# Two graph layers on one core: layer 0's row-by-entry matrix kept as bytes, and the seams around it reordered

## The chip, the cores and the metric

The kernel runs on one core of a Trainium2 chip. The metric is the device time of one execution in microseconds (us). The core's engines each run their own queue in order: TensorE (PE; PEld is its loading of weights), VectorE (DVE), ScalarE (ACT), GpSimd (POOL) and SyncE (SP). ACT, POOL and SP also issue DMAs, which share the core's 16 DMA engines.

## The reference

Input x is 4096 rows of 512 numbers, adj a 4096 by 4096 matrix of 0 and 1 that is about one in a thousand ones. Cut to what matters:

```python
# layer 0: attention with 8 heads over the neighbours in adj
Wh = einsum('nf,hfo->hno', x, W)
e  = leaky_relu(f1[:, :, None] + f2[:, None, :], 0.2)   # f1 = Wh.a[:64], f2 = Wh.a[64:]
e  = where(adj > 0, e, -9e15)
x  = layernorm(x + heads_side_by_side(softmax(e) @ Wh))
# layer 1: own row and mean of the neighbours
agg = (adj > 0) @ x / max(deg, 1)
out = concat(x @ W_self + b_self, agg @ W_nb + b_nb) @ W_comb + b_comb
x   = layernorm(x + relu(out))
```

## The kernel before

The 4096 rows are 32 blocks of 128. adj is not multiplied with anything: it is read once, and each row's few neighbours are turned into a list of column numbers. Both layers then gather their neighbours' rows from tables in HBM (t0 for layer 0, t1 for layer 1) with indirect DMAs. A block gathers 5 sets of 128 rows: the first three neighbours of each row (K0 = 3), and two sets of 128 shared entries (KH = 2) that hold the fourth and further neighbours of whatever rows have them. The order of all work is written out by hand: every engine runs its instructions in the order in which the code issues them.

**The adj stage** (loop at L778 over blocks 0 to 29). load_adj (L366) requests a block of adj as two half-blocks of 1 MB each on SP's queue; there are four buffers, so two blocks are under way. mask_adj (L375) turns a half-block into bf16 on ACT (L377). key_bank (L381) puts column numbers into a PSUM bank, fold_adj (L389) multiplies the masks with powers of two into the bank (L395), max_keys (L405) takes each row's largest keys on DVE (L410). Beside this, transposed (L307) turns a block of x (L311 on PE, the copy xT at L313 on ACT), node_block (L755) makes that block's table row (L319 on PE, copies to SBUF at L323 on DVE, two row buffers), and store sends it to t0.

**decode** (L412) works on four blocks at a time and is a generator, whose parts other work is put between. Part A (L417 to L430) unpacks keys; part B (L434 to L438) takes each block's sixteen largest; part C (L440 to L450) makes degrees and the first three indices; part D (L452 to L469) makes, for each of the four blocks, the 128 by 256 row-by-entry matrix (L465, L466), which says which row owns which shared entry; part E multiplies it with the lists (L473) and makes the shared entries' indices. With slow=True, used for the last four blocks, part D is split by block. "some(lists)" runs one part of each pending decode; in the loop each iteration runs one.

**The seam before layer 0** (L812 to L858): the last two node blocks, the masks and keys of blocks 30 and 31 (LB = 30), the gathers of blocks 0 and 1, the product of W_nb with the lower half of W_comb into m2 (fold_weights, L252: transposes L259, matmuls L270, copies L261 and L273), the last decode up to part C, and fold_bias (L276), which multiplies b_nb with the same half of W_comb on PE (L285) and adds it to a row of the bias on DVE (L289).

**Layer 0** (loop at L864). Step i works on several blocks at once: moments and normalizing of block i (L611, L618 to L627), the product with m2 of block i-1 (a_z, L632, its input turned by L311 and L313) and its store to t1, the weighted sums of block i+1, and the weights of block i+2. a_owners (L507) makes the entry-by-row matrix of a block from its lists; a_owned (L529) transposes it on PE (L532) and copies the result from PSUM to the tile st on ACT (L534); a_reach (L564) multiplies st with the reciprocal sums (L568), which the weights in a_normed need. Parts D and E of the last decode run in steps 2 to 6. Gathers go out of five buffers (GA = 5).

**The seam before layer 1** (L903 to L939): fold_weights for W_self into m1, fold_bias for b_self, spread_bias (L292), which spreads the one bias row over 128 rows by a matmul (L295).

**Layer 1** (loop at L941): gathers from t1 out of seven buffers, the product with m1 (L656), the shared entries (L663), the bias, normalizing (root, norm) and the store to the output.

Of the kernel before, what the change touches and what calls it, by code (L numbers as in the profile page):

```python
# [46 lines left out]
U32 = mybir.dt.uint32  # L47

K0 = 3
KH = 2  # L50
# [36 lines left out]
def listed_layers(  # L87
# [115 lines left out]
    oner = const.tile([1, P], F32, name="oner")  # L203
    nc.vector.memset(oner, 1.0)
# [13 lines left out]
    f1s = const.tile([P, NB, KS, H], F32, name="f1s")  # L218
    idx = const.tile([P, NB, KS], U32, name="idx")
# [32 lines left out]
    def fold_weights(loaded, m, wp, tag):  # L252
# [12 lines left out]
        for c in range(FB):  # L265
# [3 lines left out]
            for d in range(FB):  # L269
                nc.tensor.matmul(  # L270
                    mp, lhsT=wT[:, d, :], rhs=wc[:, d, :], start=(d == 0), stop=(d == FB - 1)
                )
            nc.scalar.copy(m[:, c, :], mp)  # L273
            wT = nxt

    def fold_bias(loaded, brw):  # L276
# [3 lines left out]
        bcol = small.tile([P, FB], F32, name="bcol", bufs=1)  # L280
        nc.scalar.copy(bcol, bt)
        yield
        bp = ps.tile([1, HD], F32, name="sm", bufs=2)
        for d in range(FB):
            nc.tensor.matmul(  # L285
                bp, lhsT=bcol[:, d : d + 1], rhs=loaded[1][:, d, :],
                start=(d == 0), stop=(d == FB - 1),
            )
        nc.vector.tensor_add(brow[0:1, :], bp, brow[0:1, :])  # L289
        yield  # L290

    def spread_bias():  # L292

        bp = ps.tile([P, HD], F32, name="sm", bufs=2)
        nc.tensor.matmul(bp, lhsT=oner, rhs=brow[0:1, :], start=True, stop=True)  # L295
# [38 lines left out]
    def mean_row(w_sb, xacc, wp):  # L334
# [9 lines left out]
        mr = wp.tile([P, HD], F32, name="y", bufs=2)  # L344
# [15 lines left out]
        nc.scalar.dma_start(t0[1:2, H:TW], mr[0:1, :])  # L360
# [5 lines left out]
    def load_adj(b, ap, hs=range(NH)):  # L366

        for h in hs:
# [6 lines left out]
    def mask_adj(b, h, ap):  # L375
        ab = masks[b, h] = ap.tile([P, NG // NH, SC], BF16, name="ab", bufs=3)
# [35 lines left out]
    def decode(b0, dp, place, slow=False):  # L412
# [26 lines left out]
        yield  # L439
# [21 lines left out]
        for b in range(b0, b0 + G):  # L461
# [4 lines left out]
            nc.vector.scalar_tensor_tensor(st, io, off, lt, OP.is_ge, OP.mult)  # L466
            sts.append(st)
# [61 lines left out]
    def a_owned(b, wp):  # L529
        tq = ps.tile([P, KH, P], F32, name="sm", bufs=2)  # L530
        for k in range(KH):
            nc.tensor.transpose(tq[:, k, :], OWN[b][:, k, :], ident)  # L532
        ST[b] = wp.tile([P, KH, P], F32, name="st", bufs=2)
        nc.scalar.copy(ST[b], tq)  # L534
# [157 lines left out]
    dp = ctx.enter_context(tc.tile_pool(name="decode", bufs=1, side="right"))  # L692
    fp_cm = tc.tile_pool(name="fold", bufs=1, side="right")
    fp = fp_cm.__enter__()
    ap_cm = tc.tile_pool(name="lists", bufs=1, side="right")
# [25 lines left out]
    for k in range(2):  # L721
        pa.append(ps.tile([P, HD], F32, name=("sm", "key")[k], bufs=(2, 1)[k]))
        nc.tensor.matmul(pa[k], lhsT=oner, rhs=av[0:1, k], start=True, stop=True)
# [50 lines left out]
    for h in range(NH):  # L774
        mask_adj(0, h, ap)
# [581 lines left out]
```

## Time and profile before

| what | value |
|---|---|
| median of three runs | 719.69 us (718.86 to 720.13) |
| the profiled execution: its run | 720.06 us |
| the profiled execution: its span | 718.4 us |
| mean granted TensorE clock | 0.965 of full speed |
| busy: PE, DVE, ACT, POOL | 646.3, 488.8, 443.7, 360.5 us |
| layer 0, 300 to 400 us: PE, DVE, ACT, POOL busy | 97.44, 92.43, 62.37, 65.79 of 100 us |
| layer 1, 600 to 700 us: PE, DVE, ACT, POOL busy | 100.00, 59.29, 72.09, 75.63 of 100 us |
| adj stage, 100 to 200 us: DMA | 392 GB/s |

A line of the timeline or of the groups gives the engine, the line of the kernel, the operation and "out<-in" by the names of tiles, then shapes; in a timeline it begins with the start and the duration in us, and in brackets stands how long the engine had been idle before it and what ended that. "issue" means that nothing shown was waited for. A busy PE is not a PE at its peak, since the ends of matmuls are modelled.

### The profile page before, as it was taken

The numbers are of one execution on the slowest core, as the hardware profiler recorded it, in microseconds if no ns is written. First come the engines' busy times: TensorE is split into PE (matmuls) and PEld (weight loads), VectorE is DVE, ScalarE is ACT, GpSimd is POOL, SyncE is SP. The second block draws the span as 40 slices with busy tenths as digits, with TensorE's granted clock in tenths as the row PEclk, the third lists the DMA queues.
The fourth block names the chain that finished last, engine by engine and source line by source line (L and its number), as shares of the span: only waits on it lengthen the run. The fifth ranks groups of instructions, "written<-read, shape, count | busy, mean of one in ns | idle before, by whom it ended". The sixth has DMA issues, their size and how long they took to land. (4 is left out here: it accounts for less than half of the span.)

```text
span 718.4 us, 9039 instructions
## 1 busy us (share of the span) xinstructions
PE 646.3 (90%) x2534; PEld 365.2 (51%) x2534; DVE 488.8 (68%) x1424; ACT 443.7 (62%) x915; POOL 360.5 (50%) x403
## 2 busy tenths in 40 slices
PE   4797888887999769999999999999999999999992
PEld 2465666655676335555555555554344444444440
DVE  5266777875876378999999999981116665566553
ACT  3567777676784315556666576664237777677764
POOL 6512222121002476566666666400777777777770
PEclk9989999999999978999999999999989999999997
DMA  9999999999997676977877887611667888888883
GB/s 282 389 352 394 393 393 394 393 391 392 390 391 265 216 211 204 316 213 206 231 228 231 232 227 230 185 44 45 200 203 245 258 254 260 254 258 258 262 255 108
DMA packets 84263, 191.28 MB, mean 266 GB/s; under 512 B 12513, under 2 KB 12521, under 8 KB 84206
## 3 DMA queue, kind: packets, MB, share of 16 engines
q0 software_dynamic: 25600, 84.56, 40.2%
q1 hardware_dynamic: 53952, 97.53, 37.0%
q10 hardware_dynamic: 4654, 8.54, 3.1%
q8 instruction: 22, 0.36, 0.2%
q14 instruction: 35, 0.29, 0.1%
HBM read 165.29 MB, written 25.31 MB: 265 GB/s over the span
## 5 line engine op out<-in xcount | busy, mean ns | idle before, releaser
L515 POOL DMA_INDIRECT g<-t,idx x320 | 304.4, 951 | 172.4 <-issue 120.2
L377 ACT ACTIVATE ab<-at 128x2048 bf16<-128x2048 int32 x64 | 122.3, 1911 | 55.8 <-DMA at<-in_adj_dram 49.6
L319 PE MATMUL pw<-w_sb,xT 128*128 128x264 f32 x512 | 133.4, 407 | 1.0 <-DVE row L323 0.9
L632 PE MATMUL pw<-m,xT 128*128 128x512 f32 x256 | 118.0, 604 | 3.1 <-ACT xT L313 1.7
L319 PEld LDWEIGHTS pw<-w_sb,xT 128*128 128x128 f32 x512 | 96.4, 198 | 29.3 <-issue 4.7
L313 ACT COPY xT<-tp 128x512 f32<-128x512 f32 x80 | 46.3, 579 | 91.5 <-PE tp L311 89.8
L305 POOL TENSOR_TENSOR xacc<-xacc,xs 128x512 f32<-128x512 f32 x32 | 41.1, 1284 | 122.6 <-DMA xs<-in_x_dram 122.0
L583 DVE TENSOR_TENSOR g<-g,key 128x1024 f32<-128x1024 f32 x64 | 77.9, 1217 | 1.1
L632 PEld LDWEIGHTS pw<-m,xT 128*128 128x128 f32 x256 | 46.1, 190 | 55.3 <-issue 45.8
L595 PE MATMUL nm<-g,own 128*128 128x512 f32 x128 | 66.3, 643 | 0.0
L656 PE MATMUL nm<-m,xT 128*128 128x512 f32 x128 | 60.4, 617 | 1.3 <-ACT xT L313 1.3
L311 PEld LDWEIGHTS tp<-ident,xs 128*128 128x128 f32 x320 | 40.9, 148 | 36.1 <-issue 29.8
L656 PE MATMUL pw<-m,xT 128*128 128x512 f32 x128 | 57.6, 593 | 0.0
L311 PE MATMUL tp<-ident,xs 128*128 128x128 f32 x320 | 50.6, 283 | 6.0 <-DMA xs<-in_x_dram 5.8
L323 DVE COPY row<-pw 128x264 f32<-128x264 f32 x64 | 27.1, 425 | 33.3 <-PE pw L319 23.9
L656 PEld LDWEIGHTS nm<-m,xT 128*128 128x128 f32 x128 | 24.1, 199 | 26.1 <-issue 24.6
L670 DVE SCALAR_TENSOR_TENSOR sm<-y,lst,nm 128x512 f32<-128x512 f32 x16 | 12.1, 755 | 36.7 <-PE nm L663 36.6
L670 DVE SCALAR_TENSOR_TENSOR sm<-y,lst,pw 128x512 f32<-128x512 f32 x16 | 12.1, 755 | 34.3 <-PE pw L663 34.3
L656 PEld LDWEIGHTS pw<-m,xT 128*128 128x128 f32 x128 | 23.2, 191 | 23.4 <-issue 23.4
L663 PE MATMUL pw<-g,own 128*128 128x512 f32 x64 | 31.4, 615 | 3.0 <-DMA g<-t,idx 3.0
L595 PEld LDWEIGHTS nm<-g,own 128*128 128x128 f32 x128 | 23.1, 200 | 16.9 <-issue 16.1
L549 PEld LDWEIGHTS sm<-e,own 128*128 128x128 f32 x128 | 19.8, 199 | 22.7 <-ACT e L543 11.6
(178 smaller groups left out, 1031.1 us busy)
## 6 DMA issues: line engine op xcount, KB each, us to landing
at<-in_adj_dram SPq DMA_DIRECT2D x64, 1024.0 KB, 11.2
t<-row SPq DMA_DIRECT2D x32, 256.0 KB, 3.6
out_dram<-row SPq DMA_DIRECT2D x32, 256.0 KB, 3.8
t<-row ACTq DMA_DIRECT2D x31, 260.0 KB, 6.0
xs<-in_x_dram SPq DMA_DIRECT2D x31, 256.0 KB, 11.5
g<-t,idx POOLq DMA_INDIRECT x320, 4.1
wc<-in_L_gnn_W_comb_dram SPq DMA_DIRECT2D x2, 1024.0 KB, 14.8
w_sb<-in_L_gnn_W_dram SPq DMA_DIRECT2D x8, 128.0 KB, 4.4
```

The source lines that it names most:

```text
L305: nc.gpsimd.tensor_tensor(xacc, xacc, xs[:, b, :], OP.add)
L311: nc.tensor.transpose(tp[:, c, :], xs[:, b, ts(c, P)], ident)
L313: nc.scalar.copy(t, tp)
L319: nc.tensor.matmul(pw, lhsT=xT[:, c, :], rhs=w_sb[:, c, k * HW : (k + 1) * HW], start=(c == 0), stop=(c == FB - 1),)
L323: nc.vector.tensor_copy(row[:, k * HW : (k + 1) * HW], pw)
L377: nc.scalar.activation(ab, loads.pop((b, h)), AF.Relu, accum_out=asum[:, b, h : h + 1])
L515: nc.gpsimd.indirect_dma_start(out=g[:, k, 0 : table.shape[1]], out_offset=None, in_=table[:, :], in_offset=bass.IndirectOffsetOnAxis(ap=i ...
L583: nc.vector.tensor_tensor(gv if to is None else to.rearrange("p (k h d) -> p k h d", k=1, h=H), gv, E[b][:, sl].unsqueeze(3).to_broadcast( ...
L595: nc.tensor.matmul(NM[b], lhsT=OWN[b][:, k, :], rhs=G0[b][:, K0 + k, H:TW], start=False, stop=(k == KH - 1), skip_group_check=True,)
L632: nc.tensor.matmul(pz, lhsT=xT[:, c, :], rhs=m2[:, c, :], start=(c == 0), stop=(c == FB - 1))
L656: nc.tensor.matmul(NM[b], lhsT=xT[:, c, :], rhs=m1[:, c, :], start=False, stop=False, skip_group_check=True,)
L663: nc.tensor.matmul(NM[b], lhsT=OWN[b][:, k, :], rhs=g[:, K0 + k, 0:HD], start=False, stop=(k == KH - 1), skip_group_check=True,)
```

## The change

In decode, each row-by-entry matrix is also copied to bytes by ACT, into a new tile "of" for all 32 blocks. In layer 0, a_owned no longer transposes: it copies the bytes back to numbers, from SBUF. Part B of a slow decode is split by block. fold_weights stops twice for each of its four column blocks where it stopped once. The bias: a column of b_nb or b_self is made once (bias_column), fold_bias multiplies it with the half of W_comb on DVE and adds up in all 128 rows of brow (cleared at block 3), and one matmul with ones sums the rows and spreads the result (sum_bias). The mean row uses a row buffer instead of a y buffer. Both halves of block 30 are requested in the loop, and block 30's masks run before the last fold of the loop's blocks. The buffers of adj and of the masks are pools of their own, and layer 0's small tiles come from a new pool (wq). In the seam and in layer 0's loop the order is as in the diff.

```diff
+    of = const.tile([P, NB, KH * P], U8, name="of")
...
                 nc.tensor.matmul(
                     mp, lhsT=wT[:, d, :], rhs=wc[:, d, :], start=(d == 0), stop=(d == FB - 1)
                 )
+            yield
             nc.scalar.copy(m[:, c, :], mp)
...
+    def bias_column(k, brw):
         bt = ps.tile([P, FB], F32, name="sm", bufs=2)
         nc.tensor.transpose(bt, brw, ident[0:FB, 0:FB])
...
+    def fold_bias(loaded, bcol):
         for d in range(FB):
-            nc.tensor.matmul(
-                bp, lhsT=bcol[:, d : d + 1], rhs=loaded[1][:, d, :],
-                start=(d == 0), stop=(d == FB - 1),
-            )
-        nc.vector.tensor_add(brow[0:1, :], bp, brow[0:1, :])
+            nc.vector.scalar_tensor_tensor(
+                brow, loaded[1][:, d, :], bcol[:, d : d + 1], brow, OP.mult, OP.add
+            )
-    def spread_bias():
+    def sum_bias():
         bp = ps.tile([P, HD], F32, name="sm", bufs=2)
-        nc.tensor.matmul(bp, lhsT=oner, rhs=brow[0:1, :], start=True, stop=True)
+        nc.tensor.matmul(bp, lhsT=ones, rhs=brow, start=True, stop=True)
         nc.scalar.copy(brow, bp)
...
-        mr = wp.tile([P, HD], F32, name="y", bufs=2)
+        mr = wp.tile([P, FW], F32, name="row", bufs=2)
...
             nc.vector.max(nb[:, g, 8:16], kj[:, g, :])
-        yield
+            if slow or g == G - 1:
+                yield
...
             nc.vector.scalar_tensor_tensor(st, io, off, lt, OP.is_ge, OP.mult)
+            nc.scalar.copy(of[:, b, :], st)
...
     def a_owned(b, wp):
-        tq = ps.tile([P, KH, P], F32, name="sm", bufs=2)
-        for k in range(KH):
-            nc.tensor.transpose(tq[:, k, :], OWN[b][:, k, :], ident)
         ST[b] = wp.tile([P, KH, P], F32, name="st", bufs=2)
-        nc.scalar.copy(ST[b], tq)
+        nc.scalar.copy(ST[b].rearrange("p k c -> p (k c)"), of[:, b, :])
...
-            load_adj(LB, ap, (0,))
+            load_adj(LB, ap)
         if b == 3:
             brw = load_bias(1)
+            nc.vector.memset(brow, 0.0)
...
+        if b == 5:
+            bcol = bias_column(1, brw)
...
     row = node_block(w, xT)
     store(w, row)
+    key_bank(LB)
+    for h in range(NH):
+        mask_adj(LB, h)
     fold_adj(LB - 1, dp)
     max_keys(LB - 1)
     row = node_block(w + 1, nxt)
     store(w + 1, row, nc.sync)
-    load_adj(LB, ap, (1,))
     load_adj(LB + 1, ap)
...
     m2s = fold_weights(loaded, m2, wp, "pw")
-    next(m2s)
-    mask_adj(LB, 0, ap)
-    some(lists)
-    next(m2s)
-    key_bank(LB)
-    mask_adj(LB, 1, ap)
-    some(lists)
-    next(m2s)
     some(lists)
     fold_adj(LB, dp)
     max_keys(LB)
-    a_owners(0, wp)
-    a_owned(0, wp)
-    mask_adj(LB + 1, 0, ap)
     next(m2s)
     key_bank(LB + 1)
-    mask_adj(LB + 1, 1, ap)
+    some(lists)
+    for k in range(3):
+        next(m2s)
+    mask_adj(LB + 1, 0)
+    a_owners(0, wp)
+    fold_bias(loaded, bcol)
+    some(lists)
+    mask_adj(LB + 1, 1)
+    next(m2s)
     fold_adj(LB + 1, dp)
     max_keys(LB + 1)
+    next(m2s)
...
+    wq = ctx.enter_context(tc.tile_pool(name="work2", bufs=1))
+    a_owned(0, wq)
...
     lists = [decode(NB - G, dp, on_last, slow=True)]
     some(lists)
-    next(m2s, None)
-    some(lists)
-    for _ in fold_bias(loaded, brw):
-        pass
-    some(lists)
...
+        if i == -1:
+            next(m2s)
         if i >= -1 and on(i + 2):
-            a_owned(i + 2, wp)
+            a_owned(i + 2, wq)
...
+        if i == -2:
+            next(m2s)
+            some(lists)
...
+        if i == -1:
+            next(m2s, None)
-        if 2 <= i < 8:
+        if 2 <= i < 12:
             some(lists)
...
+    bcol = bias_column(0, brw)
+    fold_bias(loaded, bcol)
     for _ in fold_weights(loaded, m1, wp, "nm"):
         pass
-    for _ in fold_bias(loaded, brw):
-        pass
-    spread_bias()
+    sum_bias()
```

## The prediction

> **What bounds the kernel now.** I read the busy table by stretches first, then the timeline of each seam, the waits, and the chain that ended last. Three stages show: up to about 224 us the stream of adj (388 to 395 GB/s in every window from 60 to 215 us); layer 0 to 498 us; layer 1 to the end.
>
> The chain of waits that ended last, and the waits in layer 1 (engine, tile, line, released by: us, times, longest):
> ```profile
> 698.63 1.00 POOL g L515
> 699.94 5.19 DMA g<-t,idx
> 705.27 3.26 PE pw L663 x4
> ```
> ```profile
> POOL g L515 <- issue: 81.5, 132, 41.6
> ```
> ```profile
> PE pw L663 <- DMA g<-t,idx: 3.0, 1, 3.0
> ```
> Layer 1 ends with the last gather. The 41.6 is the gap to 501.88 us, where layer 0's last rows have landed; from there POOL issues 160 gathers with no other wait worth a name, (699.63-501.88)/160 = 1.24 us each. TensorE looks 100% busy there, yet it waited 3.0 us for the last gather. **So layer 1 is POOL's, and the end moves one for one with the end of layer 0.**
>
> A steady step of layer 0, on the timeline (start, us, engine):
> ```profile
> 405.10 0.60 PE L311 MATMUL tp<-ident,xs 128*128 128x128 f32 x4
> 405.53 0.51 PE L568 MATMUL sm<-dn,st 128*128 128x8 f32 x4
> 405.73 0.58 ACT L313 COPY xT<-tp 128x512 f32<-128x512 f32 x1 [2.02 <-PE tp L311]
> 405.90 0.42 PE L532 MATMUL sm<-ident,own 128*128 128x128 f32 x2
> 406.37 0.30 PEld L632 LDWEIGHTS pw<-m,xT 128*128 128x128 f32 x2 [0.29 <-ACT xT L313]
> ```
> The step is 6.97 us (L611 at 405.30 and 412.27). Its z matmuls (L632) start when ACT's xT copy ends (405.73+0.58 = 406.31), and ACT starts that copy as soon as L311 is done. The transposes to be removed (L532) stand inside that copy's time.
>
> The seam between the stages:
> ```profile
> 224.88 1.07 ACT L261 COPY xT<-sm 128x512 f32<-128x512 f32 x2 [7.33 <-DVE row L323]
> 225.52 3.70 PE L270 MATMUL pw<-wc,xT 128*128 128x512 f32 x8 [0.29 <-ACT xT L261]
> ```
> ```profile
> 246.73 0.61 PE L395 MATMUL nm<-ab,fold 128*32 128x512 bf16 x6 [1.53 <-ACT ab L377]
> 247.45 0.89 DVE L410 MAX8 kk<-nm 128x8 f32<-128x128 f32 x4 [9.29 <-PE nm L395]
> 255.34 0.68 DVE L289 TENSOR_TENSOR brow<-sm,brow 1x512 f32<-1x512 f32 x1 [0.60 <-PE sm L285]
> ```
> ```profile
> 258.89 1.02 PE L568 MATMUL sm<-dn,st 128*128 128x8 f32 x4 [0.49 <-DVE dn L562]
> ```
> From the last node block's matmuls (224.35) to layer 0's first reach (258.89) pass 34.5 us in which no engine is full: DVE waits 9.3 us for the keys of block 31, which ACT masks late, and TensorE then does the bias. This seam is what the change works on.
>
> **The change part by part.** *The transposes.* Removed: two L532 matmuls a step (0.42 us) and a copy from PSUM (L534, 0.37); added: a copy from bytes, also on ACT. As z waits for xT, I take 0 per step. The other end: were z released earlier, the step could shrink to VectorE's own 6.80 (L611 at 329.23, 336.03, 342.83), 0.17 in each of the 18 steps from 356.47 to 482.04, 3.2 us. A copy to or from bytes has no row; its nearest are L534 (0.37, 256 wide) and L313 (0.58, 512 wide), so 0.3 to 0.6 us; I take 0.4, as the width is L534's. In a steady step it hides in ACT's 2.02 us of waiting.
>
> *The seam.* Both halves of block 30 are now requested before the row stores, its masks run before the last node blocks, the fold of m2 is cut finer, and the bias goes to VectorE. TensorE's new chain after 224.35: about 0.9 for the second mask, then L395 0.6, eight L259 transposes 1.0, L270 3.7, four L259 0.6, L270 3.7, L473 1.9, L259 0.6, L395 for block 31 0.6: 13.6, to 237.9. VectorE then has the keys (0.9, with 0.2 of latency) and decode part A (248.38 to 251.37, 3.0), and from the first L539 to the reach is 1.9 (257.02 to 258.89), plus 0.4 for what does not hide of the first quarter of part B: 6.4. Reach at 244.3 instead of 258.89: **-14.6**. Four products of 128x512 for the bias (row L611, 0.69 each, 2.8 us) run while L270 does; the third L270 runs beside VectorE's keys and decode, the fourth behind the reach, where TensorE waits anyhow. Without that cover each would cost 3.7 more. Block 31's two masks (4.1 us of ACT) follow the first copy of m2 and end near 237.1; their data is requested at about 225.3 as before, with 1 MB less ahead of it. On SP the second half of block 30 is now requested ahead of the last row store; it waits for a mask of block 28, long done by 224.85, when that store goes, so the store keeps its time: 0. The new clearing of the bias row holds ACT's DMA at block 3 until VectorE gets there; the pads' clearing holds it there already (VectorE 41.56, ACT's DMA 42.09): 0.
>
> *The clock.* In 2 us windows (columns: PE, PEld, DVE, ACT, POOL busy, granted clock, DMA share, GB/s):
> ```profile
> 256.00:258.00 2.00, 0.22 (x2) 0.22 (x3) 1.48 (x10) 0.24 (x1) 1.54 (x2) 1.00 0.80 223
> 260.00:262.00 2.00, 0.43 (x2) 0.03 (x1) 1.93 (x5) 1.10 (x3) 1.39 (x3) 0.50 0.73 202
> 272.00:274.00 2.00, 2.00 (x3) 0.74 (x3) 1.39 (x6) 0.00 (x0) 0.92 (x1) 0.50 0.76 218
> ```
> Half speed from 259 to 275 lengthens the first steps: L611 of blocks 0, 1 and 2 starts 7.8 us after the reach, 8.66 and 7.22 later. With L270 kept in that stretch and no gap over 1.5 us I expect full speed: 7.0, 6.97 and 6.97, **-2.7** (bounds 0 and -2.7). The Trainium skill (TensorE: Matmul & The Clock Gate, Part 1: The HAM clock gate) speaks against taking work off TensorE: it says an idle window of about 3.4 us halves the clock. By that rule the emptier bias and transposes would risk the 2.7; by the row the work moved into the gap matters more.
>
> *Decode in layer 0's loop.* The last decode (blocks 28 to 31) leaves three quarters of part B (0.81 each) and part C (1.1) to loop steps: 3.5 us of VectorE. VectorE has 6.97-6.80 = 0.17 spare a step, so over four more steps **+2.8** (bounds 0 if TensorE is behind anyhow, and 3.5). In the four steps that build the matrix, the byte copy waits for VectorE and holds the xT copy behind it on ACT: z comes 1.45 us later once, and the last decode step, 8.74 us long (L611 313.70 to 322.44), takes it up. I take 0; the other end is 1.45.
>
> *The adj stage.* Every fourth iteration four byte copies now stand on ACT ahead of the xT copy, the row store, the key copy and both masks, and wait for VectorE:
> ```profile
> 204.90 0.59 ACT L313 COPY xT<-tp 128x512 f32<-128x512 f32 x1 [0.76 <-PE tp L311]
> 206.38 1.91 ACT L377 ACTIVATE ab<-at 128x2048 bf16<-128x2048 int32 x1 [0.39 <-DMA at<-in_adj_dram]
> 208.16 0.48 DVE L466 SCALAR_TENSOR_TENSOR own<-iota,lst,lt 128x256 f32<-128x256 f32 x1
> 212.94 0.62 PE L395 MATMUL key<-ab,fold 128*32 128x512 bf16 x8
> ```
> The fourth matrix is done at 208.64, so the masks after it start near 210.3 and end near 214.4, 1.5 us past where L395 wanted them, and TensorE has no gap here (from 184.8 to 219.5). The group one earlier (matrices done at 183.3) gives 2.0 in the same way. The four earlier groups are free: adj is requested about 11 us before it lands, and between 30 and 215 us ACT sat idle 50.4 us before its masks (44.2 of it for DMA), 1.9 for each of 27 iterations, which takes up 2 to 3 us of lateness before the next group. The mean row's tile now shares the two row buffers: the next row's copy waits for a store to land (the same wait cost 3.27 us at 45.33 with the pads), moving VectorE's matrices 2 us later. It all adds to 2.0+1.5+2 less what overlaps: I take **+4.0**, bounds 0 and 5.4. That also delays the gathers of blocks 0 and 1 (228.04, 13 us for ten, some 5 more to land); they would arrive near 250.5, just past need: **+0.5** (0 to 2).
>
> *The layer 1 seam.* The bias leaves TensorE (514.18 to 519.35, 5.2 us). POOL hides that: 0; without POOL's cover, up to -5.2.
>
> **Sum:** -14.6 - 2.7 + 2.8 + 4.0 + 0.5 = -10.0. The profiled execution has span 718.4 and run 720.06 us (1.7 outside it), 0.4 over the median of 719.69. So span 708.4, and beside the median **709.7 us**; its own bounds some 705 to 714.
>
> **The rivals.**
> *The step shrinks, or the adj stage is not held up.* For: ACT waits for DMA all through. Against: TensorE's gapless run there, and the xT copy. No hold (-4.0), half of the 3.2 gained: 704. Chance 0.15.
> *The clock stays low and the hold is long.* For: the gaps at 241 to 243 and before the second step's reach. No clock gain, hold 5.4, late gathers 2: 709.7+2.7+1.4+1.5 = 715. Chance 0.11.
> *Slower: the copies starve the adj stream.* Place: the six groups inside the stream, ACT's order. Price: if each leaves the DMA queues empty for 3 us, 18 us in place of 4.0: 724. It decides from 14.0/6 = 2.3 us a group, and ACT's lateness would have to exceed the cushion of 11.2-2.7 = 8.5 us (landing time less one half-block's own). Against: masks slip by 3 to 4 us only. Chance 0.10.
> *The change does not do what it says:* the transposes go but the seam's order is undone by some wait of block 30's masks for memory: about 719.7. Chance 0.02.
> The forecast has 0.62.
>
> **How the numbers follow.** From 702 (full gain without hold, most of 3.2) to 718 holds the forecast, nearly all of its neighbours and leaves the slower case out. About 0.2% is what a measurement here tells from no change: faster 0.87, same 0.02, slower 0.11.
>
> **What would show it.** In the changed profile: no L532, the step still near 6.97 with z waiting for xT; reach of block 0 near 248 and clock 1.00 after it; decode parts B in loop steps of 7.4 to 7.8; the last node block near 228; z of block 31 some 10 us earlier, and from there the same 160 gathers at 1.24. The forecast falls if DMA drops below 380 GB/s in 60 to 210 us, if POOL shows waits for buffers, or if the reach is not before 252.

## The result, and the profile after

| | before | after |
|---|---|---|
| median, us (7 runs each) | 719.69 (718.46 to 721.61) | 717.0 (713.19 to 719.84) |
| ratio, 95% interval | | 0.9958 (0.9934 to 0.9982) |
| profiled execution: run / span, us | 720.06 / 718.4 | 717.85 / 716.1 |
| last node block's matmuls end | 224.4 | 227.8 |
| first reach (L568 before, L569 after) | 258.89 | 250.69 |
| first moment of layer 0 (L611, L612), then blocks 0 to 2, 2 to 11, 11 to 31 | 266.7; 15.88, 67.03, 138.94 | 259.5; 17.09, 73.06, 138.12 |
| last moment of layer 0, and from there to the end of the span | 488.6; 229.8 | 487.8; 228.3 |

The kernel is 2.7 us faster where 10 were forecast; the time lies in the range. The table already says where the rest went: 8.2 us are won up to the reach, and all of them are given back in layer 0's first eleven steps (block 11's moment is at 349.6 us in both kernels). The 0.8 by which layer 0 ends earlier come behind that.

The chain that ended last (start, us, engine) and layer 1's waits, after:
```profile
697.96 0.95 POOL g L519
...
699.21 4.84 DMA g<-t,idx
...
704.18 1.97 PE pw L664 x4
```
```profile
POOL g L519 <- DVE brow L290: 41.6, 1, 41.6
...
PE nm L664 <- DMA g<-t,idx: 5.9, 2, 5.0
```
Layer 1 is still POOL's: the last gather starts 0.7 us earlier, as layer 0 ends 0.8 earlier, and the 41.6 us gap ahead of the first gather has not shrunk. TensorE, freed of the bias, now waits 7.9 us for gathers (5.9 with nm, 2.0 with pw) where it waited 3.0. The other 1.6 us of the end are the last gather's landing and four matmuls at a higher clock (1.97 for 3.26; granted 1.00 from 704 to 706 us, and 0.50 from 706 to 708 in the kernel before). Nothing in the change aims at these; they are luck.

A steady step after (timeline of TensorE):
```profile
404.29 0.60 PE L313 MATMUL tp<-ident,xs 128*128 128x128 f32 x4
404.73 0.51 PE L569 MATMUL sm<-dn,st 128*128 128x8 f32 x4
405.57 3.70 PE L633 MATMUL pw<-m,xT 128*128 128x512 f32 x8 [0.33 <-ACT xT L315]
```
The transposes are gone, and in their place TensorE waits 0.33 us for ACT's xT. The step is 6.98 us (L313 at 404.29 and 411.27): their removal is worth nothing here.

The seam, on VectorE and TensorE:
```profile
230.31 0.89 DVE L412 MAX8 kk<-key 128x8 f32<-128x128 f32 x4 [0.78 <-PE key L397]
...
239.51 0.48 DVE L511 TENSOR_SCALAR own<-iota,es 128x128 f32<-128x128 f32 x2 [3.47 <-PE sm L477]
239.91 3.11 DVE L290 SCALAR_TENSOR_TENSOR brow<-wc,bcol,brow 128x512 f32<-128x512 f32 x4
...
244.44 0.88 DVE L412 MAX8 kk<-nm 128x8 f32<-128x128 f32 x4
```
```profile
235.44 3.60 PE L272 MATMUL pw<-wc,xT 128*128 128x512 f32 x8
238.88 1.86 PE L477 MATMUL sm<-lst,own 128*128 128x24 f32 x16
...
241.15 0.76 PE L397 MATMUL nm<-ab,fold 128*32 128x512 bf16 x8
241.84 3.70 PE L272 MATMUL pw<-wc,xT 128*128 128x512 f32 x8
249.17 1.02 PE L550 MATMUL sm<-e,own 128*128 128x8 f32 x4 [3.64 <-ACT e L544]
250.69 1.02 PE L569 MATMUL sm<-dn,st 128*128 128x8 f32 x4 [0.49 <-DVE dn L563]
251.56 5.72 PE L272 MATMUL pw<-wc,xT 128*128 128x512 f32 x8
```
The wait of 9.29 us for block 31's keys is gone. A new one stands ahead of the bias: the four "own" buffers still hold the matrices that L477 has to read, and L477 stands on TensorE behind m2's second column (L272 at 235.44). So VectorE, which has the bias row's 3.11 us behind that wait, takes block 31's keys at 244.44, 2.5 us after TensorE has made them (241.15 + 0.76). TensorE then has nothing for 3.64 us, and the same L272 that took 3.70 takes 5.72. The windows of 2 us (PE, PEld, DVE, ACT, POOL busy, granted clock, DMA share, GB/s) show why:
```profile
246.00:248.00 2.00, 0.00 (x0) 0.00 (x0) 1.85 (x6) 0.00 (x0) 1.39 (x3) 1.00 0.77 223
248.00:250.00 2.00, 0.83 (x4) 0.83 (x4) 1.61 (x8) 1.11 (x4) 1.70 (x2) 0.72 0.65 177
...
252.00:254.00 2.00, 2.00 (x3) 0.71 (x3) 1.97 (x4) 0.24 (x1) 1.70 (x2) 0.50 0.80 225
...
260.00:262.00 2.00, 0.00 (x0) 0.00 (x0) 1.83 (x7) 1.61 (x6) 1.43 (x2) 1.00 0.75 216
262.00:264.00 2.00, 1.51 (x5) 1.36 (x6) 1.97 (x4) 1.04 (x3) 1.66 (x2) 0.63 0.74 216
...
268.00:270.00 2.00, 1.98 (x5) 1.37 (x6) 1.29 (x2) 1.98 (x5) 1.40 (x2) 0.50 0.70 216
```
Both empty TensorE windows are followed by a lower clock, 0.72 and 0.63 in the next window and 0.50 behind it. The kernel before had a gap ahead of its first L549 too, behind the bias:
```profile
251.71 3.59 PE L285 MATMUL sm<-wc,bcol 128*1 128x512 f32 x8 [0.59 <-ACT bcol L281]
257.78 0.61 PE L549 MATMUL sm<-e,own 128*128 128x8 f32 x4 [2.48 <-ACT e L543]
```

The byte copies, in the adj stage (with the mean row's wait) and in layer 0's loop:
```profile
205.33 0.43 DVE L325 COPY row<-pw 128x264 f32<-128x264 f32 x1 [4.66 <-DMA t<-row]
```
```profile
208.96 0.40 ACT L470 CAST of<-own 128x256 uint8<-128x256 f32 x1 [4.04 <-DVE own L469]
...
212.99 1.91 ACT L379 ACTIVATE ab<-at 128x2048 bf16<-128x2048 int32 x1
...
315.78 0.41 ACT L470 CAST of<-last 128x256 uint8<-128x256 f32 x1 [4.24 <-DVE last L469]
316.09 0.58 ACT L315 COPY xT<-tp 128x512 f32<-128x512 f32 x1
```
```profile
316.72 5.40 PE L633 MATMUL pw<-m,xT 128*128 128x512 f32 x8 [2.11 <-ACT xT L315]
```
ACT waits with the copy for VectorE's matrix, and the mask or the xT copy behind it waits along. In the loop z starts 2.11 us late, and it runs for 5.40 us instead of 3.70, at a granted clock of 0.50 between 318 and 320 us. That step takes 8.66 us and the last decode step 10.16 (8.74 before).

### The profile page after: what moved, and what is told of

Its sections match the earlier page's. It is cut to its first block, busy times and chain, and to the rows that moved or that the text cites. A ratio compares the mean times of both kernels' runs of the same rounds, so it can differ in the third digit from the quotient of the medians.

```text
span 716.1 us, 8935 instructions
## 1 busy us (share of the span) xinstructions
PE 636.6 (89%) x2454; PEld 362.1 (51%) x2454; DVE 492.2 (69%) x1431; ACT 453.3 (63%) x947; POOL 361.6 (50%) x403
## 5 line engine op out<-in xcount | busy, mean ns | idle before, releaser
L321 PE MATMUL pw<-w_sb,xT 128*128 128x264 f32 x512 | 137.9, 417 | 0.1
L633 PE MATMUL pw<-m,xT 128*128 128x512 f32 x256 | 122.1, 621 | 12.3 <-ACT xT L315 12.3
L321 PEld LDWEIGHTS pw<-w_sb,xT 128*128 128x128 f32 x512 | 99.1, 204 | 29.0 <-issue 3.6
L596 PE MATMUL nm<-g,own 128*128 128x512 f32 x128 | 64.5, 628 | 0.0
L313 PEld LDWEIGHTS tp<-ident,xs 128*128 128x128 f32 x320 | 40.5, 147 | 38.3 <-issue 31.5
L657 PE MATMUL nm<-m,xT 128*128 128x512 f32 x128 | 57.7, 593 | 1.5 <-ACT xT L315 1.5
L313 PE MATMUL tp<-ident,xs 128*128 128x128 f32 x320 | 50.9, 284 | 7.9 <-DMA xs<-in_x_dram 7.4
L657 PE MATMUL pw<-m,xT 128*128 128x512 f32 x128 | 57.6, 592 | 0.0
L664 PE MATMUL nm<-g,own 128*128 128x512 f32 x64 | 32.0, 625 | 5.9 <-DMA g<-t,idx 5.9
L647 DVE TENSOR_TENSOR sm<-sm,g 128x512 f32<-128x512 f32 x32 | 22.2, 694 | 19.5 <-ACT sm L643 19.5
## 6 DMA issues: line engine op xcount, KB each, us to landing
at<-in_adj_dram SPq DMA_DIRECT2D x64, 1024.0 KB, 10.7
```

Of the source, the lines that this page charges most:

```text
L313: nc.tensor.transpose(tp[:, c, :], xs[:, b, ts(c, P)], ident)
L321: nc.tensor.matmul(pw, lhsT=xT[:, c, :], rhs=w_sb[:, c, k * HW : (k + 1) * HW], start=(c == 0), stop=(c == FB - 1),)
L596: nc.tensor.matmul(NM[b], lhsT=OWN[b][:, k, :], rhs=G0[b][:, K0 + k, H:TW], start=False, stop=(k == KH - 1), skip_group_check=True,)
L633: nc.tensor.matmul(pz, lhsT=xT[:, c, :], rhs=m2[:, c, :], start=(c == 0), stop=(c == FB - 1))
L657: nc.tensor.matmul(NM[b], lhsT=xT[:, c, :], rhs=m1[:, c, :], start=False, stop=False, skip_group_check=True,)
L664: nc.tensor.matmul(NM[b], lhsT=OWN[b][:, k, :], rhs=g[:, K0 + k, 0:HD], start=False, stop=(k == KH - 1), skip_group_check=True,)
```

## The experiments

All are edits of the changed kernel, except e_after, which is that kernel itself, and e_before, which is the kernel before. Three of the chips they ran on behave otherwise than that of the result: there the kernel before itself takes 797 us. So the traces are compared stretch by stretch, with the same marks as in the table above. Line numbers in the expectations are the changed kernel's, and MM1 is the product that makes m2 (L272).

| kernel | node matmuls end | first reach | first moment | blocks 0 to 2 | 2 to 11 | last moment | to the end | median | ratio to before (95%) |
|---|---|---|---|---|---|---|---|---|---|
| *before near 797* | | | | | | | | | |
| e_before | 223.9 | 256.73 | 267.3 | 15.30 | 69.20 | 501.3 | 288.3 | 796.74 | 1.0023 (0.9998 to 1.0049) |
| e_after | 227.2 | 266.99 | 276.4 | 14.69 | 77.47 | 518.6 | 288.0 | 803.62 | 1.0109 (1.0061 to 1.0158) |
| e_own | 228.2 | 254.35 | 268.1 | 18.22 | 78.63 | 511.8 | 288.0 | 799.64 | 1.0029 (0.9999 to 1.0059) |
| e_late | 226.3 | 264.89 | 274.5 | 15.26 | 70.98 | 505.6 | 286.8 | 795.84 | 0.9941 (0.9896 to 0.9987) |
| e_turn | 225.9 | 270.45 | 281.0 | 15.38 | 70.77 | 519.9 | 283.4 | 805.03 | 1.0082 (1.0045 to 1.0120) |
| e_mr | 226.4 | 264.76 | 274.1 | 14.14 | 77.61 | 510.8 | 287.6 | 801.79 | 1.0078 (1.0038 to 1.0118) |
| e_warm | 228.5 | 268.41 | 277.3 | 15.41 | 76.12 | 515.7 | 289.3 | 804.18 | 1.0119 (1.0077 to 1.0161) |
| e_partb | 228.0 | 267.65 | 277.0 | 14.15 | 74.93 | 511.8 | 285.3 | 800.54 | 1.0051 (1.0009 to 1.0093) |
| e_all | 223.5 | 254.32 | 267.3 | 21.23 | 71.45 | 506.9 | 288.8 | 795.63 | 0.9998 (0.9971 to 1.0026) |
| e_own2 | 226.0 | 265.96 | 275.2 | 14.58 | 77.29 | 513.7 | 286.0 | 798.3 | 1.0029 (0.9997 to 1.0060) |
| e_pace | 225.1 | 249.25 | 259.3 | 21.81 | 74.97 | 501.9 | 280.2 | 783.93 | 0.9854 (0.9814 to 0.9894) |
| e_best | 223.1 | 250.32 | 265.6 | 15.07 | 71.57 | 498.1 | 290.4 | 790.56 | 0.9948 (0.9913 to 0.9983) |
| e_win | 224.0 | 254.05 | 268.5 | 14.21 | 72.14 | 500.5 | 285.5 | 790.32 | 0.9902 (0.9863 to 0.9941) |
| e_two | 226.6 | 266.59 | 275.8 | 15.39 | 71.82 | 507.9 | 286.6 | 796.15 | 0.9979 (0.9947 to 1.0012) |
| *before at 719.51* | | | | | | | | | |
| p_warm | 226.8 | 250.83 | 257.3 | 13.79 | 72.94 | 482.1 | 241.3 | 725.11 | 1.0083 (1.0053 to 1.0114) |
| p_partb | 225.5 | 253.54 | 262.9 | 14.15 | 70.32 | 486.0 | 241.9 | 729.81 | 1.0143 (1.0111 to 1.0176) |
| p_turn | 224.4 | 251.37 | 262.1 | 14.22 | 70.65 | 485.2 | 242.3 | 730.89 | 1.0161 (1.0113 to 1.0208) |
| p_best | 223.7 | 249.79 | 257.8 | 13.52 | 70.60 | 480.0 | 241.0 | 723.6 | 1.0053 (1.0031 to 1.0076) |

The p kernels hold a pause on POOL after every block's gathers, which costs layer 1 some 12.7 us (241.0 less 228.3) and is not part of what they test. The changed kernel with the pause alone has no run on that chip, so they are compared with each other and, across chips, with the changed kernel's trace.

**The order in the seam (e_own), the byte copies (e_late, e_turn), the mean row (e_mr).**
```
e_own:      some(lists)                        # matrices of blocks 24 to 27
       +    fold_bias(loaded, bcol)
       +    some(lists)                        # L477 and es
            for k in range(3): next(m2s)
            mask_adj(LB + 1, 0); a_owners(0, wp)
       -    fold_bias(loaded, bcol)
       -    some(lists)
```
```
e_late: -       nc.scalar.copy(of[:, b, :], st)          # right behind L469
        +   [nc.scalar.copy(of[:, b0 + g, :], sts[g]) for g in range(G)]   # next part, before L477
e_mr:   -   mr = wp.tile([P, FW], F32, name="row", bufs=2)
        +   mr = bp.tile([1, HD], F32, name="mr", bufs=1)
```
e_turn leaves out the byte matrix "of" with its copies; a_owned transposes OWN[b] on TensorE and copies it from PSUM again, as in the kernel before.

> Theory: in the changed kernel VectorE stands 3.47 us at L511 of block 0 (239.51) because all four own buffers hold the matrices of decode(24) until TensorE's L477, which is queued behind two columns of MM1; bias row, es, max_keys(31) and the first part of the last decode come late by that. With L477 emitted right behind the matrices, the bias row ahead of it and L511 behind it, the wait is under 0.5 us, the first part of the last decode ends near 245.8 instead of 248.4, the first L569 starts near 248.1 instead of 250.69 (-2.6 us), TensorE's gap of 3.64 us ahead of L550 shrinks to about 1, and if that gap is what halves its clock, the granted clock at 248 to 256 stays above 0.9 and the first step gains 1 to 3 us more: time -2.5 to -5 against the changed kernel. Rival: the wait goes to another place (keys of block 31, first gathers), the first L569 stays within 0.7 us of 250.69 and the time within 0.7 us.

> Theory: the byte copies stand on ScalarE ahead of the copy of xT and of the masks and wait there for VectorE's last matrix (10.2 us of such waits in the loop, 7.7 in the last 50 us of the adjacency stage). With the four copies one decode part later (in front of L477, when the matrices are long done) ScalarE doesn't wait for L469, the last node matmuls end about 2 us earlier (near 226 instead of 227.8) and the step of 8.66 us in the loop falls to about 7.6: time -2 to -3.5 against the changed kernel. Rival: VectorE sets the order itself and ScalarE's wait hides in it: the copies in a row (4 x 0.41 us) only shift it, time within 0.7 us, the step of 8.66 stays.

> The byte matrix is left out and the two transposes per step are back; the rest of the change stays. Theory: the transposes cost nothing on TensorE in the steady steps (6.97 us, set by POOL's gathers and VectorE) and the byte copies cost some 4 to 6 us by holding ScalarE in the adjacency stage and in the loop: -3 to -6 us against the changed kernel, steady step 6.97, last node matmuls near 225.5 to 226. Rival: the first 16 steps are set by the chain through TensorE, and each transposed pair at 0.17 to 0.42 us comes back there: +3 to +6 us.

> Theory: the mean row now takes one of the two row buffers, and VectorE waits 4.66 us at L325 (205.33) for a row's store to the table, which is a piece of the 3.5 us by which the adjacency stage ends later. With a tile of its own that wait is gone and the last node matmuls end 1.5 to 2 us earlier: time -1.5 to -2. Rival: the next wait (ScalarE's byte copies, the masks) takes it over: the stage ends within 0.4 us of 227.8 and the time is the same within 0.7 us.

*Measured.* With e_late and e_turn the steps of blocks 7 to 11 are 7.58, 7.64, 7.57, 8.71 and 7.58, 7.64, 7.57, 8.74 us instead of the changed kernel's 8.66, 7.59, 7.57, 10.16: 2.4 to 2.5 us, the same in every later kernel with either edit. In e_late the copies come in a row and hold nobody; ACT's xT follows TensorE again, here in the step that ended late:
```profile
350.63 0.58 ACT L315 COPY xT<-tp 128x512 f32<-128x512 f32 x1 [2.08 <-PE tp L313]
356.02 1.32 ACT L473 CAST of<-last 128x256 uint8<-128x256 f32 x4
```
So the loop's hold is shown. In the adj stage a single repair does not stand out: the node matmuls end at 225.1 to 228.5 in kernels that don't touch that stage (e_after, e_own, e_own2, e_warm, e_partb, e_pace, p_warm, p_partb), at 226.3 and 226.6 with e_late's edit alone (e_late, e_two), at 226.4 with e_mr and at 225.9 and 224.4 without the bytes (e_turn, p_turn). The mean row and the copies repaired together reach 223.1 to 224.0 (e_all, e_best, e_win, p_best), some 3.3 us earlier than the mean of the first group. What goes with a late end is a dip of the adj stream between 180 and 200 us: it moves 345 to 377 GB/s there in all kernels whose node matmuls end at 226.3 or later, the changed kernel with 351 among them, and 385 to 393 in all that end by 226.0 (390 in the kernel before). Why it dips in some kernels with unrepaired copies and not in others is open. e_own's edit had a fault: L477 ahead of m2's columns made them, ACT's copies of them and the masks of block 31 late (keys at 247.9). The times say little, since something else holds the seam up on this chip.

**The changed kernel itself, all repairs, filled gaps, decode parts back.** e_all is e_own, e_late and e_mr together.
```
e_warm:  +    tp = ps.tile([P, FB, P], F32, name="tp", bufs=1)     # 20 before the loop,
         +    for k in range(20):                                  # 14 at i == 0 behind a_reach
         +        nc.tensor.transpose(tp[:, k % FB, :], ident, ident)
e_partb: -    some(lists)                       # ahead of the loop
         +    for k in range(4): some(lists)
         -    if 2 <= i < 12:
         +    if 2 <= i < 9:
```


> The changed kernel itself, without an edit, as the measure for the three others of this call. If the chip behaves like that of the first result: ratio 0.996 to the kernel before, last node matmuls from 227.4 us, first L569 at 250.7, part A of the loop as in the first trace. If it behaves like that of the first four experiments (kernel before near 797 us), engines stand for stretches of 4 to 27 us with nothing in the profile that they wait for, in layer 1 above all, and only stretches without these gaps can be compared.

> The three repairs at once: byte copies one decode part later, the mean row in a tile of its own, L477 and the bias row ahead of L511. Theory: they add up, since each takes another wait of the one chain: last node matmuls 3 us earlier (near 224.4 instead of 227.4), first L569 some 5.5 us earlier (near 245 instead of 250.7), the copy of xT no longer held in the loop (-1 to -2.5): time -5 to -8 against the changed kernel. Rival: they share one wait (the matrix loads or the gathers on POOL set the stretch from 224 to 250): -1.5 to -3.

> 20 transposes of the identity ahead of the first L550 and 14 behind the second L569, in TensorE's gaps of 3.64 and 2.70 us; nothing reads them. Theory: the clock falls to 0.50 at 249 to 255 and 263 to 273 because of these gaps, so with them filled it stays at 1.0, L272 takes 3.7 instead of 5.72 us, L596 1.96 instead of 3.76, the first L633 3.7 instead of 5.72, and since these stand on the path of the first steps the time falls by 2.5 to 5 us against the changed kernel. Rival: the clock is as predicted, but VectorE sets the first steps, so the time falls by under 1 us; or the clock doesn't answer to the filled gaps at all, and nothing changes or the filling costs up to 1 us.

> Three of the decode's parts (L438 to L440 of three blocks, 0.81 us each on VectorE) are put back from the loop's steps into the seam. Theory: VectorE sets both the seam and the steps 2 to 11, so moving its work between them is worth nothing: the first L569 comes about 2.5 us later, blocks 2 to 11 take about 2.5 us less than the 73 us of the first trace, time within 1 us of the changed kernel. Rival (the prediction's way of counting: the seam gains all, the loop has room): time +2 to +2.5 us.

*Measured.* Unchanged, the kernel is slower than before on this chip (1.0109), and its first moment comes at 276.4 instead of 259.5. From its trace, VectorE and POOL:
```profile
255.23 0.16 DVE L559 TENSOR_REDUCE dn<-e 128x8 f32<-128x24 f32 x1
266.54 0.16 DVE L562 TENSOR_TENSOR dn<-dn,sm 128x8 f32<-128x8 f32 x1 [11.15 <-remote]
```
```profile
262.05 0.95 POOL L519 DMA_INDIRECT g<-t,idx  x1 [0.30 <-issue]
276.62 0.94 POOL L519 DMA_INDIRECT g<-t,idx  x1 [13.62 <-PE nm L596]
```
L562 needs L550, which the trace shows from 254.81 for 1.02 us; VectorE goes on 11 us later, 3.5 us after POOL's last gather has been issued. The gaps cover what e_warm and e_partb were to show in time (804.18 and 800.54, against 803.62 for e_after). A part can still be read: in e_warm the second L596 takes 1.96 us behind the filled gap (3.63 in e_after).

**A mended order, all repairs with one filled gap, the kernel before, a pause on POOL.** e_own2 puts the bias row and L477 behind m2's first column instead of ahead of it; e_best is e_late, e_mr, e_own2 and the 14 transposes.
```
e_pace:  def gather(...):  ...
         +    nc.gpsimd.memset(cols, 0.0)       # behind the five gathers of a block
```


> e_own put L477 ahead of MM1's columns and so made the columns, ScalarE's copies of them and the masks of block 31 4 us late (keys at 247.9 instead of 241.9). Here L477 and the bias row stand behind the first column and ahead of the second. Theory: L511's wait of 3.47 us is under 0.5, es (L481) is written by 240 to 241 instead of 242.9 to 243.9, the keys of block 31 stay at 241 to 243, the last decode's first part ends 2 to 2.6 us earlier than with the order of the changed kernel. Time -2 to -3 us where nothing else holds the seam up (kernel before near 719), unclear within 3 us where it does (kernel before near 797). Rival: the keys move later again and the gain is under 0.7 us.

> Byte copies one part later, mean row in a tile of its own, the order of e_own2, and 14 transposes of the identity that nothing reads behind the second L569. Theory: last node matmuls from 223.2 to 223.6 (e_all: 223.2), the loop's steps with the byte copies at 7.6 and 8.7 us instead of 8.66 and 10.16, first L596 after the gap 1.96 instead of 3.6 to 3.8 us: on a chip where the kernel before takes 719, 707 to 711; where it takes 797, 792 to 795. Rival: as e_all, 795.6 or ratio 1.000 there, since what the seam gains is held up behind the gathers.

> The kernel before itself, for its trace on this chip. Theory: layer 1 (from the last moment of layer 0 to the end) takes as long as in all the variants here, 283 to 289 us against 229.8 in the trace of before, so the difference between the two kernels on this chip comes from the stretch from 224 to 280 us: there the changed kernel has the kernel before's work in another order and engines stand 4 to 15 us behind matmuls that the profile shows as ended. The first moment of layer 0 (266.7 in the trace of before) comes some 8 to 10 us before e_after's 276.4. Rival: layer 1 is the one that differs.

> POOL clears an unused 128 x 512 bf16 tile after the five gathers of each block, under 1 us; the rest is the changed kernel. Theory for the long gaps on this chip: while POOL issues gathers back to back, signals from TensorE reach the other engines 5 to 12 us late, until POOL pauses (gaps of 9 to 11 us every 22 us in layer 1, each ends 3 us after POOL stops). With a pause after each block the gaps in layer 1 shrink and layer 1 takes 235 to 265 instead of 288 us: time 745 to 785. Rival: the gaps have another cause, the pauses come on top: 805 to 830. Where the chip shows no such gaps (kernel before near 719): 717 plus 32 pauses in layer 1, 730 to 750.

*Measured.* In e_own2 L511's wait is gone, es is written at 238.18 instead of 242.93, and TensorE has block 31's keys at 242.78 to 243.4; VectorE goes on at 247.73 only. e_pace takes such gaps out of the seam with one instruction a block (POOL, then TensorE):
```profile
242.88 0.54 POOL L525 MEMSET cols<- 128x512 bf16 x1
243.58 0.95 POOL L519 DMA_INDIRECT g<-t,idx  x1 [0.17 <-issue]
```
```profile
249.25 1.02 PE L570 MATMUL sm<-dn,st 128*128 128x8 f32 x4 [0.49 <-issue]
```
The first reach is at 249.25, against 265.96 in e_own2 on the same chip, and the time 783.93 (two runs) against 798.3. The gap is not gone everywhere: the step behind the first moment takes 12.83 us (7.15 in e_after). Layer 1 took 280.2 us, not the 235 to 265 of the expectation. With the pause it takes 241.0 on a chip like the first (p_best), so 39 of the 60 us by which this chip lengthens it are something else. e_before: layer 1 is the same for both kernels on such chips (288.3 and 288.0), so what makes the changed kernel lose there is the seam, 9.1 us at the first moment, and the loop, 8.3 from block 2 to 11. These two traces come from two chips and overstate it: they are 17.3 us apart at the last moment, the medians 6.9.

**The open terms with the pause, on a chip like the first.** Each p kernel is the e kernel of the same name with e_pace's line.

> e_warm with the pause of e_pace. Theory of the clock: the 20 transposes fill TensorE's 3.69 us gap ahead of the first L550 and the 14 the gap behind the second L569, so the first L550 takes 0.5 to 0.6 us instead of 1.02, MM1's last column 3.7 instead of 5.50, the second L596 1.96 instead of 3.76, the first moment of layer 0 comes 1.5 to 2.5 us earlier (near 257.3 instead of 259.3) and the stretch up to the third moment 2 to 4 us earlier than in e_pace (281.1). Rival: the clock stays up but VectorE sets these steps: first moment within 0.5 us of 259.3.

> e_partb with the pause of e_pace, so that the seam can be read too. Theory: three parts of 0.81 us moved from the loop back into the seam: first L569 2.4 to 3.3 us later than e_pace's 249.25 (251.6 to 252.6), three of the loop's steps 6.8 instead of 7.6 us, layer 0's last moment within 1 us of 501.9 where the unexplained gaps are alike. Rival (the prediction's count, in which the seam's gain was whole): the seam loses 2.4 to 3.3 and the loop gains nothing: 504.3 to 505.2.

> e_turn with the pause of e_pace: no byte matrix, the transposes of each step back on TensorE. Theory: the adjacency stage 1.9 us shorter and the loop's steps with parts D and E 1.1 and 1.4 us shorter, transposes free in the steady steps: layer 0's last moment 3 to 5 us earlier than e_pace's 501.9, time 778 to 781. Rival: the transposes come on the path of the seam and of the first steps (0.17 to 0.42 us in each of some 16 steps): 0 to +3 us, 784 to 787.

> e_best with the pause of e_pace (POOL clears an unused tile after each block's gathers). Theory: the four repairs keep their worth when the seam isn't held up: last node matmuls near 223.4, first L569 at 243 to 246 (e_pace: 249.25), first moment of layer 0 at 251 to 255 (e_pace: 259.3), loop some 2.5 us shorter than e_pace's 242.6 and about 3 more where the first steps keep their clock, so layer 0's last moment at 489 to 495 instead of 501.9, time 770 to 777. Rival: what is won up to 250 us is lost in the first steps to the gathers (POOL issues five blocks' worth in a row): 781 to 784.

*Measured.* p_warm, TensorE's timeline and one window:
```profile
245.89 2.35 PE L867 MATMUL tp<-ident 128*128 128x128 f32 x20
249.69 0.61 PE L551 MATMUL sm<-e,own 128*128 128x8 f32 x4 [1.45 <-ACT e L545]
250.83 0.61 PE L570 MATMUL sm<-dn,st 128*128 128x8 f32 x4 [0.52 <-DVE dn L564]
251.29 3.68 PE L272 MATMUL pw<-wc,xT 128*128 128x512 f32 x8
```
```profile
268.00:270.00 2.00, 2.00 (x8) 0.99 (x8) 1.86 (x4) 0.58 (x1) 1.42 (x2) 1.00 0.74 215
```
The reach is where it was in the changed kernel's trace (250.83, 250.69), but block 2's moment comes 20.3 us behind it instead of 25.9. On the same chip and with the same pause p_partb, with both gaps open, needs 23.5 and has its clock at 0.50 at 250 to 258 us. So the clock is worth 3.3 us between these two, and up to 5.6 against the changed kernel's trace.

p_partb: the reach 2.85 us later than in the changed kernel, blocks 2 to 11 shorter by 2.74. Moving the parts is worth nothing within what these traces can tell, as its theory had it.

p_turn: blocks 2 to 11 shorter by 2.4, steady steps the same 6.97 to 6.98, but the first moment 10.7 us behind the reach (8.8 in the changed kernel). ACT's copy there waits for the transposes behind m2's column, and the exponentials behind the copy wait with it:
```profile
258.54 0.37 ACT L537 COPY st<-sm 128x256 f32<-128x256 f32 x1 [8.16 <-PE sm L536]
```
Against p_partb, whose gaps are open too and where the first moment is 9.4 us behind the reach, that is 1.3 us. So the bytes are worth 1.3 to 1.9 us in the seam and cost 2.4 in the loop.

p_best: the node matmuls end at 223.7, 4.1 us before the changed kernel's, and the reach is only 0.9 earlier, at 249.79 where 243 to 246 were expected. Its trace shows what takes the place of the repaired waits, ACT's mask of block 30, VectorE and TensorE:
```profile
223.71 1.91 ACT L379 ACTIVATE ab<-at 128x2048 bf16<-128x2048 int32 x1 [2.60 <-DMA at<-in_adj_dram]
...
226.97 1.91 ACT L379 ACTIVATE ab<-at 128x2048 bf16<-128x2048 int32 x1 [1.26 <-DMA at<-in_adj_dram]
```
```profile
230.16 0.90 DVE L412 MAX8 kk<-key 128x8 f32<-128x128 f32 x4 [4.73 <-PE key L397]
...
243.95 0.89 DVE L412 MAX8 kk<-nm 128x8 f32<-128x128 f32 x4 [2.79 <-PE nm L397]
```
```profile
229.02 1.04 PE L397 MATMUL key<-ab,fold 128*32 128x512 bf16 x6 [2.86 <-ACT ab L379]
229.99 1.97 PE L261 MATMUL sm<-ident,wr 128*128 128x128 f32 x8
...
231.82 4.79 PE L272 MATMUL pw<-wc,xT 128*128 128x512 f32 x8
```
VectorE waits 4.73 us for block 30, whose second half only landed at about 227, and 2.79 us for block 31. The stage of adj is a stream of data, and its end sets block 30's keys (230.16 here, 230.31 in the changed kernel) whether the node blocks are done early or late. And TensorE, with its node blocks done early, now waits 2.04 and 2.86 us for the masks; at a granted clock of 0.50 from 228 to 234 us its L261 and first L272 take 1.97 and 4.79 us, where the changed kernel's took 1.09 and 3.68. So some 2.0 us of the repair are lost to the clock before block 31's keys.

**A version without the pause.** e_win is e_best with six transposes ahead of the first L550 as well; e_two is e_late with e_warm's filled gaps.

> All repairs without the pause: byte copies one part later, mean row in its own tile, L477 behind MM1's first column, 6 transposes of the identity ahead of the first L550 and 14 behind the second L569. From the traces with the pause (first moment 257.8 with a half-clock L272 of 5.38, last moment of layer 0 at 480.0): with the first gap filled as well the last moment at 478 to 480, layer 1 as in the first trace of the changed kernel (228.3), time 707 to 711 where the kernel before takes 719 (ratio 0.983 to 0.989). Rival: without the pause the gaps behind the gathers return and it is within 3 us of the changed kernel, 714 to 720. Where the kernel before takes 797: 787 to 793.

> Two repairs alone: the byte copies one part later and the filled gaps (20 and 14 transposes). Theory: these two, -2.4 us in the loop and -5.6 us in the first steps, are nearly all that the forecast missed; the mean row and L511 don't set the seam's end, since block 31's matrix and keys do. Last moment of layer 0 at 479.5 to 480.5, time 708 to 711 where the kernel before takes 719, within 1.5 us of e_win. Rival: the mean row and L511 add up with the rest: 2 to 4 us behind e_win.

*Measured,* where the kernel before takes 798.54: e_win 790.32, faster than the kernel before (0.9902, 0.9863 to 0.9941); e_two 796.15 (0.9979, 0.9947 to 1.0012), its first moment at 275.8 against 268.5. So there e_win's repairs of the mean row and of the order count, contrary to e_two's theory, or its six transposes instead of 20 do: these runs don't separate them, and the gaps of these chips stand in both traces. On a chip like that of the result neither has run without the pause. An estimate from p_best's trace: 480.0 to the last moment, 228.3 of layer 1 and 1.7 outside the span make 710; p_warm's in the same way 712.

## Why the prediction was wrong

The forecast was right in sign and in what bounds layer 1 and the steady steps, and wrong in size: 10.0 us in the span became 2.3. By its own steps, in us:

| step | forecast | measured | what the runs showed |
|---|---|---|---|
| seam with the adj hold and the late gathers | -14.6 + 4.0 + 0.5 = -10.1 | -8.2 | hold there, +3.5 in this trace, but hardly on the path; the seam's gain itself smaller |
| the clock, reach to block 2 | -2.7 | +2.2 | full speed did not come; with the gaps filled -3.4 |
| decode in the loop, blocks 2 to 11 | +2.8 | +6.0 | parts 3.5, and the hold of xT 2.5 where 0 was taken |
| transposes, blocks 11 to 31 | 0 | -0.8 | steady step unchanged; six steps behind the decode 0.8 shorter together, as the decode ends later; p_turn, which keeps the transposes, takes 138.25 as well |
| layer 1 | 0 | -1.5 | POOL hides the bias; the last gather's landing and the clock behind it -1.6, the gathers +0.1 |
| sum | -10.0 | -2.3 | |

**The clock is the step that failed**, by 4.9 of the 7.7 us that are missing. "With L270 kept in that stretch and no gap over 1.5 us I expect full speed": the gaps were 3.64 and 2.70, and the clock was 0.50 behind both. The first gap follows from a wait that the prediction did not have: the four bias products were to run while L270 does, but VectorE stood 3.47 us at L511 ahead of them and so came 2.5 us late to block 31's keys. In p_best, without that wait, the gap is 1.01 us. In the kernel before TensorE had the bias there until 255.30, and then a gap of 2.48 us. The second gap, ahead of the second step's L550, had no number in the forecast; in the kernel before it is 2.85 us. The rival "the clock stays low" named it, at a chance of 0.11.

The Trainium skill (TensorE: Matmul & The Clock Gate, Part 1: The HAM clock gate) was weighed against this step and had the side of the risk right: it lets the clock halve after an idle window of about 3.4 us, which the first gap exceeds. The rows go further than the rule as the prediction put it: the gap of 2.48 in the kernel before, that of 2.70, and the wait of 2.11 us in the loop, were followed by 0.50 as well, and in p_best the last column of m2 still took 5.38 us behind gaps of 1.01 and 0.62 us. That p_warm needs 20.3 us from reach to block 2, where the forecast had 7.0 + 6.97 + 6.97 = 20.9, shows that the price was right and its condition was not. How much of the 4.9 us is the clock stays open within bounds: p_partb less p_warm gives 3.3, the changed kernel less p_warm 5.6.

**The xT hold was seen and set to 0.** The text named the mechanism (the byte copy holds xT behind it), took 0 because the last decode step would take it up, and gave 1.45 as the other end. It cost 2.5: 1.1 at the first of the four matrices, and 1.4 in the very step that was to absorb it, which grew from 8.74 to 10.16 us. That it halved the clock for one z is a price the sum had no term for. The moved parts came to their full 3.5 rather than 2.8, as these steps had no spare 0.17: VectorE sets them. Since VectorE sets the seam as well, the move is worth nothing (p_partb), and the sum should have booked it on both sides: 3.5 less in the seam, 3.5 more in the loop.

**The seam.** The hold of the adj stage was forecast at 4.0 and measured at 3.5 (0.7 to 4.6 in the kernels that keep it, against 224.4 and 223.9 of the kernel before), and yet p_best, which takes it away, wins 0.9 at the reach. The data of block 30 land at 227, so VectorE's first keys could not come much before 229 (229.26 in p_turn at the earliest). So +4.0 was about the right size, but hardly belonged in the sum, and the -14.6, which began at the end of the node matmuls, was too large: without a hold it puts the reach at 244.3, and p_best, without a hold, has it at 249.79, 9.1 before the kernel before. The 5.5 us between the two can be found: the forecast let block 30's second mask end 0.9 us behind 224.35, at 225.25, but its data landed at 226.97 and L397 ran at 229.02, 3.8 late; the clock behind that wait took 2.0 more. L511's 3.47 us behind L477 in the changed kernel were not in the prediction either; taking them away brings block 31's keys into their place.

Right were: layer 1 as POOL's, with the bias hidden; 0 for the transposes; POOL with no new wait. The adj stream held in the main (387 GB/s from 60 to 210 us, 392 before), but its dip to 351 from 180 to 200 us is some 2 us of data: the rival "the copies starve the adj stream" came about in one place. Of the rivals, "the clock stays low and the hold is long" (715) came nearest, at the measured 717.0, though through the loop rather than the hold.

## What to carry to other kernels

Work that is moved from one stretch to another gains only if another engine sets the second stretch: ask of both ends, and book it on both sides of the sum. Work taken off TensorE leaves a gap, so price the clock behind it too. A small copy inserted in a queue costs what stands behind it for as long as it waits for its input; put it one part later, when the input is long there.

## What the chip showed that was not expected

The same kernel took 719 us where the result was measured and on the p kernels' chip (the record doesn't say whether these are two) and 797 on three others. On the three, VectorE and ACT stood up to 15 us, and in one wait early in layer 1 up to 27, behind matmuls that the trace shows as done, mostly with no release recorded ("remote"), in stretches where POOL issued gathers back to back: in the seam, and in layer 1, which took 283 to 290 us instead of 228 to 230. The other traces have no such wait. A clearing of 0.54 us on POOL after each five gathers removed the gap ahead of the reach (249.25 for 265.96); layer 1, its pauses included, went to 280.2 only and kept a "remote" wait of 23.6 us. The cause is open. The sign of the change turned there: the changed kernel, faster by 0.4% on the first chip, was slower by 1.1% (1.0061 to 1.0158).

Filled gaps keep the clock: 20 transposes that nothing reads took 2.35 us and brought a matmul group of 5.72 us back to 3.68 (p_warm). Where a longer gap followed the filler, as in e_warm (14.79 us), the group took 5.82.
